# An LSTM with a residual on one core: weights loaded through several queues, scales per half of the state, a two-deep split and 512-wide input products

## The chip, the cores and the metric

The kernel runs on one core of a Trainium2 chip. The core has five engines that run side by side, each on its own stream of instructions and in order: PE (TensorE, matrix products), DVE (VectorE), ACT (ScalarE), POOL (GpSimd) and SP (SyncE). PE, DVE and ACT do nearly all of the work here; SP, ACT and POOL can start DMA transfers between device memory (HBM) and on-chip memory (SBUF). Products are summed in PSUM banks. The metric is the time of one execution on the device in microseconds (us); lower is better.

## What is computed

The reference is an LSTM over 512 steps for 16 sequences with 512 features and 512 hidden units, whose outputs are added to its input:

```python
xW = jnp.einsum('ntd,dg->ntg', x, Wx) + b        # 16 x 512 x 2048

def step(carry, xw_t):
    prev_h, prev_c = carry
    a = xw_t + prev_h @ Wh                       # Wh: 512 x 2048
    i = jax.nn.sigmoid(a[:, :Hdim])
    f = jax.nn.sigmoid(a[:, Hdim:2 * Hdim])
    o = jax.nn.sigmoid(a[:, 2 * Hdim:3 * Hdim])
    g = jnp.tanh(a[:, 3 * Hdim:])
    next_c = f * prev_c + i * g
    next_h = o * jnp.tanh(next_c)
    return ((next_h, next_c), next_h)
...
x = x + hs
```

Everything is float32. `x` is (16, 512, 512), the first h is `cond_1024` (16, 512), the first c is zero. A step needs the h of the step before, so the 512 steps are a chain.

## The kernel before

**Precision.** Wh is split into three float16 parts `wq0`, `wq1`, `wq2` (`split`, L377 to L387): a part is rounded on ACT, the remainder is taken on DVE, and so on. A power-of-two scale S, with its reciprocal RS, keeps the parts in range. It is found per partition from the largest absolute value (`amax`, L360, then nine small operations up to L375). h is likewise written in float16 parts (`parts`), scaled by S (the `scale` operation, L258), and the history of h is scaled back by RSL on ACT (`unscale`, L299). The first step alone multiplies float32 h by float32 Wh (`first_products`, L193).

**Tiles.** A product has the 32 columns of a small stationary operand (h or x, transposed) and streams 256 columns of weights. Four such products, j = 0 to 3, run side by side in the four column groups of the array and write partitions 32j to 32j+31. The state is handled in two halves, a and b, and each half's gates have two PSUM banks, used in alternate steps. The input product x Wx of two steps at a time, q, goes to one of four `xb` banks, started with the bias (`put_bias`, L147, on ACT), added up by `project` (L157, on PE) in two halves e of 256 columns, and copied into the gates' banks by `seed` (L167, on ACT) two steps ahead.

**Order.** Nothing is scheduled automatically. Each engine runs what is issued to it in the order of the program text. `STEP_PE` gives PE's order in a step: eight products for each of twelve names such as `q3aa` (part 3 of Wh, half a of h, gates of half a), then `x0` to `x3`, four input products each, for the pair of steps that begins four steps later, or three. `STEP` gives the order of DVE and ACT: turn the gates (`turn`, a transpose on DVE, L216), fold the parts together (`fold`, L223), tanh and sigmoid (ACT), `mix`, `cell`, tanh of the cell, then the new h in parts (`p1`, `copy`, `p2`, `rem`, `p2r`, L276 to L290) and its history (`h`, L270). Of a step's twelve names, the eighth, `q2ba`, is the last that the gates of half a need; it needs `p2r_b` of the step before (L290), the last DVE operation of half b.

**Before the first step.** SP's queue loads Wh (16 transfers of 256 KB, L128: row block c, quarter j, into partitions 32j to 32j+31), the first h (`h_in`, 4), the first block of x (`xs`, 8, L138), Wx (16) and the next x. ACT's queue loads the bias (8, L334). DVE takes the maximum of each of Wh's four row blocks c, finds the scale, turns the first h and x, and then ACT and DVE split Wh in eight pieces (4 blocks c, 2 halves e), each piece's chain started after the last one's. PE clears its eight banks with float32 products (L356), projects q = 0 and 1 as Wx lands, waits for the `seed` copies, which stand behind the split on ACT's stream, and runs the first step's products.

**At the end.** Each pair of steps p has a residual: transpose on DVE (L308), add on POOL (L309). After every fourth pair, SP writes 8 transfers of 32 KB (L315).

Of the kernel before, what the change touches and what calls it, by code (L numbers as in the profile page):

```python
# [14 lines left out]
P = 128  # L15
Q = 32
# [6 lines left out]
STEP_PE = "q3aa q3ab q1ab q1aa q2aa q3ba q1ba q2ba q2bb q1bb q2ab q3bb x0 x1 x2 x3"  # L23
# [8 lines left out]
def lstm_residual(ctx: ExitStack, tc: tile.TileContext, x, h0, wx, wh, b, out):  # L32
# [67 lines left out]
    wx_j = wx_sb.rearrange("p c (e g j w) -> p c e j g w", e=2, g=2, j=NJ)  # L100
# [4 lines left out]
    zero = const.tile([1, G * P], FP, tag="zero", name="zero")  # L105
    amax = const.tile([P, NK], FP, tag="amax", name="amax")
    top = const.tile([P, 1], FP, tag="top", name="top")
    bits = const.tile([P, 2], FP, tag="bits", name="bits")
    sc = const.tile([P, 5], FP, tag="sc", name="sc")
    S, RS, RS2, RSL = (sc[:, i : i + 1] for i in range(4))  # L110
# [13 lines left out]
    def load_w(dst, w, c):  # L124

        for j in range(NJ):
            r0 = j * P + c * Q
            nc.sync.dma_start(out=dst[j * Q : (j + 1) * Q, c], in_=w[r0 : r0 + Q])  # L128
# [3 lines left out]
    def load_xs(s):  # L132

        xs[s] = xsp.tile([P, XP, P], FP, tag="xs", name=f"xs_{s}")
        for j in range(NJ):
            for r in range(S2):
                p0 = j * Q + r * N
                nc.sync.dma_start(  # L138
                    out=xs[s][p0 : p0 + N],
                    in_=x[:, s * XB + r : (s + 1) * XB : S2, j * P : (j + 1) * P],  # L140
                )
# [4 lines left out]
    def put_bias(q):  # L146
        nc.scalar.copy(xb[q % NXB], bias)  # L147
# [6 lines left out]
    def project(q, c, e):  # L154

        for j in range(NJ):
            nc.tensor.matmul(  # L157
                xb[q % NXB][j * Q : (j + 1) * Q, (1 - e) * GU : (2 - e) * GU],
                lhsT=xT[q][:, c],
                rhs=wx_j[:, c, e, j],  # L160
                start=False,
                stop=(c == NK - 1),
                skip_group_check=True,
            )
# [75 lines left out]
    def act(t, op, h):  # L240
# [16 lines left out]
        elif op == "scale":  # L257
            nc.scalar.mul(new("os", t, h, [P, 2 * N]), v["so", h], S)  # L258
# [38 lines left out]
    def unscale(p):  # L297
        hs[p] = work.tile([P, P], FP, tag="hs", name=f"hs_{p}")
        nc.scalar.mul(  # L299
            hs[p], hist[p // XP][:, p % XP].rearrange("p c m -> p (c m)"), RSL  # L300
        )

    def residual(p):
        s, i = divmod(p, XP)
        if i == 0:
            ob[s] = outp.tile([P, XP, P], FP, tag="ob", name=f"ob_{s}")
        hb = work.tile([P, P], FP, tag="hb", name=f"hb_{p}")
        nc.vector.transpose(hb, hs[p])  # L308
        nc.gpsimd.tensor_tensor(ob[s][:, i], hb, xs[s][:, i], ALU.add)  # L309
        if i < XP - 1:  # L310
            return
        for j in range(NJ):
            for r in range(S2):
                p0 = j * Q + r * N
                nc.sync.dma_start(  # L315
                    out=out[:, s * XB + r : (s + 1) * XB : S2, j * P : (j + 1) * P],
                    in_=ob[s][p0 : p0 + N],
                )
# [4 lines left out]
    warm = const.tile([1, 1], FP, tag="warm", name="warm")  # L323
    nc.vector.memset(zero, 0.0)
    nc.vector.memset(h_in, 0.0)
    for c in range(NK):
        load_w(wh_sb, wh, c)
    for j in range(NJ):
        nc.sync.dma_start(out=h_in[j * Q : j * Q + N], in_=h0[:, j * P : (j + 1) * P])
    load_xs(0)  # L330
    b_j = b.rearrange("(o e g j w) -> j e o g w", o=1, e=2, g=2, j=NJ)
    for j in range(NJ):
        for e in range(2):
            nc.scalar.dma_start(  # L334
                out=bias[j * Q : (j + 1) * Q, (1 - e) * GU : (2 - e) * GU].rearrange(
                    "p (g w) -> p g w", g=2
                ),
                in_=b_j[j, e].broadcast_to([Q, 2, P]),
            )
    for c in range(NK):  # L340
        load_w(wx_sb, wx, c)
# [11 lines left out]
    nc.scalar.activation(warm, zero[:, 0:1], AF.Sigmoid)  # L353

    for bank in xb + gates[0] + gates[1]:
        nc.tensor.matmul(bank, lhsT=zero[:, :P], rhs=zero, start=True, stop=True)  # L356


    for c in range(NK):
        nc.vector.tensor_reduce(  # L360
            amax[:, c : c + 1], wh_sb[:, c], mybir.AxisListType.X, ALU.max, apply_absolute_value=True
        )
    nc.vector.tensor_reduce(top, amax, mybir.AxisListType.X, ALU.max)
    nc.vector.tensor_scalar(
        bits[:, 0:1].bitcast(I32), top.bitcast(I32), EXP, None, ALU.bitwise_and
    )
    nc.vector.tensor_scalar(
        bits[:, 1:2].bitcast(I32), top.bitcast(I32), EXP, EXP, ALU.bitwise_and, ALU.bitwise_xor
    )
    nc.vector.tensor_scalar(sc[:, 4:5], bits[:, 1:2], 2.0**13, 1.0, ALU.mult, ALU.min)  # L370
    nc.vector.tensor_scalar(RS, sc[:, 4:5], 2.0**-15, None, ALU.max)
    nc.vector.tensor_scalar(RS2, RS, 0.5, None, ALU.mult)
    nc.vector.tensor_scalar(RSL, RS, 1.0 / LO, None, ALU.mult)
    nc.vector.tensor_scalar(sc[:, 4:5], bits[:, 0:1], 2.0**-14, 1.0, ALU.mult, ALU.max)
    nc.vector.tensor_scalar(S, sc[:, 4:5], 2.0**15, None, ALU.min)  # L375

    def split(c, e):  # L377

        w = wh_sb[:, c, e * GH : (e + 1) * GH]
        f = [q[:, c, (1 - e) * GH : (2 - e) * GH] for q in wq]  # L380
        nc.scalar.mul(f[0], w, RS2)  # L381
        r1 = tmp.tile([P, GH], FP, tag="r1", name=f"r1_{c}_{e}")
        nc.vector.scalar_tensor_tensor(r1, w, RS, f[0], ALU.mult, ALU.subtract)  # L383
        nc.scalar.copy(f[1], r1)  # L384
        r2 = tmp.tile([P, GH], FP, tag="r2", name=f"r2_{c}_{e}")
        nc.vector.tensor_tensor(r2, r1, f[1], ALU.subtract)  # L386
        return lambda: nc.scalar.mul(f[2], r2, LO)  # L387

    nc.vector.transpose(hT0.rearrange("p c m -> p (c m)"), h_in)
    for q in range(2):  # L390
        turn_x(q)
    last = None
    for c in range(NK):
        for e in range(2):
            todo = split(c, e)
            if last:
                last()
            last = todo
            if (c, e) == (0, 0):
                for q in range(2):  # L400
                    put_bias(q)
    last()
    for q in range(2):
        for c in range(NK):
            for e in range(2):
                project(q, c, e)
    for t in range(2):
        for h in range(2):
            seed(t, h)
# [3 lines left out]
    for t in range(T):  # L413
# [4 lines left out]

        for op in STEP_PE.split():
            if op[0] == "x":  # L420
                i = int(op[1:])
                if q < NP:
                    project(q, 2 * half + i // 2, i % 2)
            elif t:
                products(t, int(op[1]), "ab".index(op[2]), "ab".index(op[3]))
            elif op[1] == "3":
                first_products("ab".index(op[2]), "ab".index(op[3]), hT0)
# [7 lines left out]
        if t % 2:  # L435
            unscale(t // 2)
# [40 lines left out]
```

## Time and profile before

| | |
|---|---|
| median of 3 runs | 2319.54 us (2317.95 to 2319.73) |
| the profiled execution: its time | 2319.52 us |
| its span, first to last instruction | 2317.7 us |
| granted TensorE clock, mean | 0.997 |
| busy: PE, PEld, DVE, ACT, POOL | 98%, 80%, 85%, 77%, 5% |
| first `turn` of the first step, last `turn_a` | at 70.42 us, at 2307.26 us |

The span is 1.8 us shorter than the execution's time. A row of the profile's groups gives line, engine, operation, tiles and shapes, the count, the busy time and the mean duration of one in ns; behind the second bar stands the engine's idle time just before, and what ended it. A row of the timeline gives start and duration in us; an idle time and its releaser stand in brackets. "PE" rows are matrix products, "PEld" rows are loads of the stationary operand, and rows on "SPq" or "ACTq" are DMA transfers being issued. A float32 product shows as two records. Products run four abreast and are pipelined, so the duration of a record is not the spacing of records.

### The profile page before, as it was taken

How to read it: one execution, taken by the hardware profiler on the slowest of the kernel's cores; microseconds unless marked ns; L12 is line 12 of the kernel's file. 1: busy time of each engine (PE TensorE's matmuls, PEld its weight loads, DVE VectorE, ACT ScalarE, POOL GpSimd, SP SyncE). 2: the span in 40 equal slices, each digit the busy share in tenths (PEclk: the TensorE clock that was granted, in tenths of full speed). 3: DMA queues.
4: the chain of work that ended last, by engine and by line, in shares of the span. 5: the costliest groups of instructions: out<-in, count | busy, mean ns of one | idle time of the engine just before them, and what ended most of it. 6: DMA issues, size and time to landing. Idle time of an engine off the chain costs nothing.

```text
span 2317.7 us, 153753 instructions
## 1 busy us (share of the span) xinstructions
PE 2263.9 (98%) x65584; PEld 1862.2 (80%) x65584; DVE 1958.8 (85%) x11808; ACT 1791.7 (77%) x7704; POOL 117.6 (5%) x264
## 2 busy tenths in 40 slices
PE   4899999999999999999999999999999999999997
PEld 1788888888888888888888888888888888888886
DVE  4788888888888888888888888888888888888887
ACT  3777777777777777777777777777777777777776
POOL 0000000000000000000000000000000000000000
PEclk9999999999999999999999999999999999999999
DMA  7000000000000000000000000000000000000000
GB/s 164 8 18 23 16 20 23 16 20 22 14 22 23 13 23 22 13 23 22 13 22 21 15 23 18 17 23 18 18 22 18 18 23 15 21 23 15 21 18 13
DMA packets 84907, 52.13 MB, mean 22 GB/s; under 512 B 17088, under 2 KB 83200, under 8 KB 83200
## 3 DMA queue, kind: packets, MB, share of 16 engines
q1 hardware_dynamic: 83584, 42.04, 7.9%
q8 instruction: 516, 8.45, 1.6%
q14 instruction: 167, 1.37, 0.2%
q10 hardware_dynamic: 640, 0.26, 0.1%
HBM read 25.46 MB, written 16.78 MB: 18 GB/s over the span
## 4 chain that ended last, share of the span: by engine, by line
PE 96%; DVE 1%; DMA 1%; ACT 1%; issue 0%; ACTq 0%; SPq 0%; POOLq 0%; POOL 0%; DVEq 0%
PE gates L180 58%; PE xb L157 38%; DMA wh_sb<-in_L_cond_Wh_dram 1%; DVE r L383 0%; ACT wq L381 0%; ACT wq L387 0%; PE gates L193 0%; ACT wq L384 0%; DMA bias<-in_L_cond_b_dram 0%; ACTq L334 0%; DVE gt L216 0%; DMA xs<-in_x_dram 0%; SPq L138 0%; DVE r L386 0%; ACT xb L147 0%
## 5 line engine op out<-in xcount | busy, mean ns | idle before, releaser
L180 PE MATMUL gates<-wq,parts 128*32 128x256 f16 x49056 | 1452.1, 273 | 5.3 <-DVE parts L276 4.2
L180 PEld LDWEIGHTS <-parts 128*32 128x32 f16 x49056 | 1306.3, 96 | 155.3 <-DVE parts L276 5.8
L157 PE MATMUL xb<-wx_sb,xT 128*32 128x256 f32 x16384 | 987.0, 380 | 27.1 <-DMA wx_sb<-in_L_cond_Wx_dram 27.1
L157 PEld LDWEIGHTS xb<-wx_sb,xT 128*32 128x32 f32 x16384 | 554.0, 110 | 270.3 <-ACT wq L381 20.2
L216 DVE STREAM_TRANSPOSE gt<-gates 128x192 f32<-128x192 f32 x1024 | 392.1, 383 | 237.0 <-PE gates L180 176.2
L250 ACT ACTIVATE gc<-pre 128x32 f32<-128x32 f32 x1022 | 235.0, 230 | 327.8 <-DVE pre L223 314.8
L167 ACT ACTIVATE gates<-xb,mask 128x256 f32<-128x256 f32 x1024 | 451.5, 441 | 0.0
L258 ACT ACTIVATE os<-so,sc 128x32 f32<-128x32 f32 x1024 | 329.1, 321 | 16.7
L280 ACT COPY parts<-parts 128x32 f16<-128x32 f16 x1022 | 214.5, 210 | 132.1 <-DVE parts L276 132.1
L223 DVE SCALAR_TENSOR_TENSOR pre<-gt 128x96 f32<-128x96 f32 x1024 | 254.2, 248 | 0.0
L252 ACT ACTIVATE sif<-pre 128x64 f32<-128x64 f32 x1024 | 245.5, 240 | 0.0
L216 DVE STREAM_TRANSPOSE gto<-gates 128x64 f32<-128x64 f32 x1024 | 230.3, 225 | 0.0
L309 POOL TENSOR_TENSOR ob<-hb,xs 128x128 f32<-128x128 f32 x256 | 116.6, 456 | 2193.6 <-DVE hb L308 1927.7
L256 ACT ACTIVATE so<-preo 128x32 f32<-128x32 f32 x1024 | 226.7, 221 | 0.0
L290 DVE SCALAR_TENSOR_TENSOR parts<-rem,parts 128x32 f16<-128x32 f32 x1022 | 196.6, 192 | 35.5
L268 ACT ACTIVATE tch<-gc 128x32 f32<-128x32 f32 x1024 | 226.3, 221 | 0.1
L223 DVE SCALAR_TENSOR_TENSOR preo<-gto 128x32 f32<-128x32 f32 x1024 | 193.0, 188 | 17.5
L282 DVE SCALAR_TENSOR_TENSOR parts<-parts,hist 128x32 f16<-128x32 f16 x1022 | 192.8, 189 | 17.7
L260 DVE TENSOR_TENSOR pr<-sif,gc 128x64 f32<-128x64 f32 x1022 | 205.6, 201 | 0.0
L276 DVE TENSOR_TENSOR parts<-os,tch 128x32 f16<-128x32 f32 x1022 | 196.7, 192 | 0.0
L266 DVE TENSOR_TENSOR gc<-pr 128x32 f32<-128x32 f32 x1024 | 192.9, 188 | 0.0
L270 DVE SCALAR_TENSOR_TENSOR hist<-os,tch 128x32 f32<-128x32 f32 x1024 | 189.6, 185 | 0.3 <-ACT tch L268 0.3
(42 smaller groups left out, 685.4 us busy)
## 6 DMA issues: line engine op xcount, KB each, us to landing
xs<-in_x_dram SPq DMA_DIRECT2D x512, 32.0 KB, 2.6
out_dram<-ob SPq DMA_DIRECT2D x512, 32.0 KB, 2.5
wh_sb<-in_L_cond_Wh_dram SPq DMA_DIRECT2D x16, 256.0 KB, 7.6
wx_sb<-in_L_cond_Wx_dram SPq DMA_DIRECT2D x16, 256.0 KB, 8.7
bias<-in_L_cond_b_dram ACTq DMA_DIRECT2D x8, 32.0 KB, 3.3
h_in<-in_cond_dram SPq DMA_DIRECT2D x4, 8.0 KB, 6.9
```

Of the source, the lines that this page charges most:

```text
L157: nc.tensor.matmul(xb[q % NXB][j * Q : (j + 1) * Q, (1 - e) * GU : (2 - e) * GU], lhsT=xT[q][:, c], rhs=wx_j[:, c, e, j], start=False, sto ...
L167: nc.scalar.mul(gates[h][t % 2][:, :GU].rearrange("p (g u) -> p g u", g=G), xb[t // 2 % NXB].rearrange("p (g h u) -> p h g u", g=G, h=2)[: ...
L180: nc.tensor.matmul(g[j * Q : (j + 1) * Q, :GU], lhsT=a[:, cc, k * N : (k + 2) * N], rhs=wq_j[i - 1][:, 2 * kh + cc, h, j], start=False, st ...
L216: nc.vector.transpose(gt.rearrange("p b m -> p (b m)"), gates[h][t % 2][:, b0 * Q : b1 * Q])
L223: nc.vector.scalar_tensor_tensor(pre.rearrange("p g (c n) -> p (g c) n", c=2), gt[:, :, (1 - t % 2) * N : (2 - t % 2) * N], 1.0 / LO, gt[: ...
L250: nc.scalar.activation(gc[h][:, 0], v["pre", h][:, 0], AF.Tanh)
L252: nc.scalar.activation(new("sif", t, h, [P, 2, 2 * N]), v["pre", h][:, 1:3], AF.Sigmoid)
L256: nc.scalar.activation(new("so", t, h, [P, 2 * N]), v["preo", h][:, 0], AF.Sigmoid)
L258: nc.scalar.mul(new("os", t, h, [P, 2 * N]), v["so", h], S)
L260: nc.vector.tensor_tensor(new("pr", t, h, [P, 2, 2 * N]), v["sif", h], gc[h], ALU.mult)
L268: nc.scalar.activation(new("tch", t, h, [P, 2 * N]), gc[h][:, 1], AF.Tanh)
L280: nc.scalar.copy(slots(t, h, 2), slots(t, h, 0))
```

## The change

- **Loads.** Wh's quarters j = 0 and 2 are issued by SP, j = 1 and 3 by ACT. The first x, then the first h, then the bias are issued by POOL. Wx is cut in two column parts, 32 transfers of 128 KB, half on SP and half on POOL, and lands with its column halves swapped; `project` takes a quarter's four runs of 128 columns in one access pattern.
- **Scale.** Instead of one scale per partition there are two, one for each half of h (row blocks 0 and 1, row blocks 2 and 3). The last block's bound is a sum of absolute values on ACT instead of a maximum on DVE.
- **Split.** A piece is in five steps (0, 2, 4 on ACT, 1, 3 on DVE), written out so that piece n+1's remainder and piece n+2's first part are issued inside piece n. Block 2's maximum is inside piece 1, block 3's bound and the second scale inside piece 2; the bias goes into `xb` inside pieces 3 and 4.
- **First step.** The input products of q = 0 and 1 are issued inside piece 4, 16 products with zeros follow them on PE, and the first step's seeds are issued inside piece 6.
- **x products.** `project` streams 512 columns instead of 256: two names per step instead of four.
- **Banks** are cleared with float16 zeros. DVE's first transposes come ahead of its first maximum.
- **End.** `unscale` has one instruction per half of h. The last pair's residual is written by itself, on SP and ACT; the three pairs before it are written when the third is done.

```diff
-STEP_PE = "q3aa q3ab q1ab q1aa q2aa q3ba q1ba q2ba q2bb q1bb q2ab q3bb x0 x1 x2 x3"
+STEP_PE = "q3aa q3ab q1ab q1aa q2aa q3ba q1ba q2ba q2bb q1bb q2ab q3bb x0 x1"
...
-    def load_w(dst, w, c):
+    def load_w(dst, w, c, dmas, parts=1):
+        n = G * H // parts
         for j in range(NJ):
             r0 = j * P + c * Q
-            nc.sync.dma_start(out=dst[j * Q : (j + 1) * Q, c], in_=w[r0 : r0 + Q])
+            for e in range(parts):
+                a = parts - 1 - e
+                dmas[j % 2].dma_start(
+                    out=dst[j * Q : (j + 1) * Q, c, a * n : (a + 1) * n],
+                    in_=w[r0 : r0 + Q, e * n : (e + 1) * n],
+                )
...
-    def project(q, c, e):
+    def project(q, c):
         for j in range(NJ):
             nc.tensor.matmul(
-                xb[q % NXB][j * Q : (j + 1) * Q, (1 - e) * GU : (2 - e) * GU],
+                xb[q % NXB][j * Q : (j + 1) * Q],
                 lhsT=xT[q][:, c],
-                rhs=wx_j[:, c, e, j],
+                rhs=wx_j[:, c, j],
...
-    def unscale(p):
...
+    def unscale(p, h):
+        if h == 0:
+            hs[p] = work.tile([P, NK, Q], FP, tag="hs", name=f"hs_{p}")
+        a = slice(2 * h, 2 * h + 2)
+        nc.scalar.mul(hs[p][:, a], hist[p // XP][:, p % XP, a], RSL[h])
...
+        if p == NP - 1:
+            put(s, i, i + 1, [nc.sync, nc.scalar])
+        elif p == NP - 2:
+            put(s, 0, i + 1, [nc.sync])
+        elif i == XP - 1:
+            put(s, 0, XP, [nc.sync])
...
+    for c in range(NK):
+        load_w(wh_sb, wh, c, (nc.sync, nc.scalar))
+    load_xs(0, nc.gpsimd)
...
-        nc.sync.dma_start(out=h_in[j * Q : j * Q + N], in_=h0[:, j * P : (j + 1) * P])
-    load_xs(0)
+        nc.gpsimd.dma_start(out=h_in[j * Q : j * Q + N], in_=h0[:, j * P : (j + 1) * P])
...
-            nc.scalar.dma_start(
+            nc.gpsimd.dma_start(
                 out=bias[j * Q : (j + 1) * Q, (1 - e) * GU : (2 - e) * GU].rearrange(
...
-        load_w(wx_sb, wx, c)
+        load_w(wx_sb, wx, c, (nc.sync, nc.gpsimd), 2)
...
+    def bound(c):
+        if c == NK - 1:
+            junk = tmp.tile([P, G * H], HP, tag="junk", name="junk", bufs=1)
+            nc.scalar.activation(junk, wh_sb[:, c], AF.Abs, accum_out=amax[:, c : c + 1])
+        else:
+            nc.vector.tensor_reduce(
...
+    def scales(h):
+        nc.vector.tensor_tensor(
+            top[:, h : h + 1], amax[:, 2 * h : 2 * h + 1], amax[:, 2 * h + 1 : 2 * h + 2], ALU.max
+        )
...
+    NH = 2 * NK
     for q in range(2):
         turn_x(q)
...
+    nc.vector.transpose(hT0.rearrange("p c m -> p (c m)"), h_in)
+    bound(0)
+    bound(1)
+    scales(0)
+    split(0, 0)
+    split(1, 0)
+    split(0, 1)
+    for n in range(NH):
+        if n == 1:
+            bound(2)
+        if n == 2:
+            bound(3)
+            scales(1)
+        if n + 1 < NH:
+            split(n + 1, 1)
+        split(n, 2)
+        split(n, 3)
+        if n + 2 < NH:
+            split(n + 2, 0)
+        split(n, 4)
+        if n in (3, 4):
+            put_bias(n - 3)
+        if n == 4:
+            for c in range(NK):
                 for q in range(2):
-                    put_bias(q)
...
+                    project(q, c)
+            for _ in range(16):
+                zeros(xb[3], False)
+        if n == 6:
+            for h in range(2):
+                seed(0, h)
+    for h in range(2):
+        seed(1, h)
     put_bias(2)
     turn_x(2)
```

`scales` has six small DVE operations behind the maximum, where the code before had eight behind its reduction; `split(n, k)` issues the same operation as before for each k.

## Prediction

> **What bounds the kernel now.** I read the page's chain first, then the groups, then timelines of three places: the loop, its last steps, the start.
>
> ```profile
> PE 96%; DVE 1%; DMA 1%; ACT 1%; issue 0%; ACTq 0%; SPq 0%; POOLq 0%; POOL 0%; DVEq 0%
> ```
>
> The chain says that the loop is PE's. It is a tie, which the last steps show, because they have no input products:
>
> ```profile
> 2290.45 1.91 PE L157 MATMUL xb<-wx_sb,xT 128*32 128x256 f32 x32
> 2292.18 2.82 PE L180 MATMUL gates<-wq,parts 128*32 128x256 f16 x96
> 2296.38 2.98 PE L180 MATMUL gates<-wq,parts 128*32 128x256 f16 x96 [1.38 <-DVE parts L276]
> 2300.75 2.98 PE L180 MATMUL gates<-wq,parts 128*32 128x256 f16 x96 [1.39 <-DVE parts L276]
> ```
>
> Without x, PE idles 1.38 us per step, yet 2296.38 to 2300.75 is 4.37. Now DVE's `turn_a`, in the middle of the run and at its end:
>
> ```profile
> 901.97 0.38 DVE L216 STREAM_TRANSPOSE gt<-gates 128x192 f32<-128x192 f32 x1 [0.38 <-PE gates L180]
> 906.33 0.38 DVE L216 STREAM_TRANSPOSE gt<-gates 128x192 f32<-128x192 f32 x1 [0.37 <-PE gates L180]
> ```
> ```profile
> 2302.90 0.38 DVE L216 STREAM_TRANSPOSE gt<-gates 128x192 f32<-128x192 f32 x1 [0.59 <-PE gates L180]
> 2307.26 0.38 DVE L216 STREAM_TRANSPOSE gt<-gates 128x192 f32<-128x192 f32 x1 [0.38 <-PE gates L180]
> ```
>
> 4.36 us with x, 4.36 without. The recurrence sets it: `turn_a`, then DVE and ACT up to `p2r_b` (3.76), then `q2ba` on PE and back (0.6). PE's own sum is next: fours of L180 records start every 0.1092 us, fours of L157 every 0.2158; 24 x 0.1092 + 8 x 0.2158 = 4.347, 15 ns under the median period of 4.362. The 511 periods from 70.42 to 2307.26 sum to 2236.84, 7.9 more than 511 x 4.362: 59 steps that run late.
>
> So what is left is 70.4 us ahead of the first `turn_a`, and 8.4 behind the last. The start's timeline:
>
> ```profile
> 0.73 4.74 ACTq L334 DMA_DIRECT2D bias<-in_L_cond_b_dram  x8
> 0.74 15.07 SPq L128 DMA_DIRECT2D wh_sb<-in_L_cond_Wh_dram  x16
> ...
> 11.02 2.29 DVE L360 TENSOR_REDUCE amax<-wh_sb 128x1 f32<-128x2048 f32 x1 [8.75 <-DMA wh_sb<-in_L_cond_Wh_dram]
> ...
> 24.92 2.29 DVE L360 TENSOR_REDUCE amax<-wh_sb 128x1 f32<-128x2048 f32 x1 [2.38 <-DMA xs<-in_x_dram]
> ...
> 28.24 1.15 ACT L381 ACTIVATE wq<-wh_sb,sc 128x1024 f16<-128x1024 f32 x1 [21.24 <-DMA xs<-in_x_dram]
> ...
> 48.36 6.58 PE L157 MATMUL xb<-wx_sb,xT 128*32 128x256 f32 x80 [2.85 <-DMA wx_sb<-in_L_cond_Wx_dram]
> ...
> 64.90 1.52 ACT L167 ACTIVATE gates<-xb,mask 128x256 f32<-128x256 f32 x4
> 65.38 5.49 PEld L193 LDWEIGHTS gates<-wh_sb,hT 128*32 128x32 f32 x128 [10.91 <-ACT gates L167]
> ```
>
> Wh is in by 24.9, the split runs from 28.2 to 65.0 (eight pieces every 4.39), the seeds wait behind it, and PE, done with x at 54.9, waits 10 us for them. The split is the path.
>
> **The change, part by part.**
>
> **Wider x.** 1024 cycles pass at once instead of twice 512. A spacing of 0.2158 is 512/2.4 GHz plus 2.5 ns, so a step's x costs 4 x 0.4292 = 1.717 instead of 1.727: 10 ns on PE. The recurrence covers all of it: 0. If PE set the period it would be 508 x 10 ns = 5.1 us gained. It can't lose while PE stays under 4.362 (4.337 now).
>
> **`unscale` in halves.** 128x128 takes 390 ns, `scale` on 128x32 321; so 128x64 about 345, twice 690: 0.3 us more on ACT in every second step. ACT idles 0.7 before its `tanh_a`, seed b behind it feeds PE a step later: 0. Exposed, it would be 256 x 0.3 = 77 us.
>
> **Wh over SP and ACT.** SP's second issue stood from 1.1 to 4.5 while ACT issued the bias; that goes, some 3.4 us. The rate is in doubt. Both ways matter: in the packets, the typical 8 KB of Wh takes 540 to 620 ns, the quickest 309, and the stream moves 1 MB per 4.66 us (225 GB/s). The Trainium skill, "SBUF — State Buffer", section "Can I just issue two DMAs to hit both halves?", speaks against the change: two transfers to different halves measured 6% more than one. By the rule Wh's first half is in at 1.8 + 2.1 MB / 239 GB/s = 10.6; by the quickest packet at about 6.5. Neither decides, as follows; I take the rule.
>
> **POOL's queue.** 8 transfers of x, 4 of h, 8 of bias, then 16 of Wx stand on it, one behind another. The trace has no DMA issued by POOL. Nearest is ACT's queue, 0.59 each (8 in 4.74). The skill's "DMA: Bandwidth & Descriptors", section "Latency and other measured facts", gives such a transfer about 1 us to its first byte, for descriptors that POOL's cores write in software. I take p = 1.0 us each, as POOL differs in kind from ACT's queue; ends 0.55 and 1.5 (the upper is my assumption). DVE's transposes of x and h now stand ahead of its maxima, so the maxima and all of the split wait for the twelfth: 0.7 + 11 x 1.0 + 3.5 to land (xs took 2.6, beside Wh more) = 15.2; at p = 0.55 it is 10.3, still behind Wh's first block. Behind the 36 issues stand only POOL's four clears of `parts` (0.7), wanted by the first step's `p1_a` at some 61: covered, unless p passes 1.6.
>
> **Start of the split.** 15.2 + 0.35 (turn h) + 2 x 2.29 (maxima) + four small operations of 0.19 = 20.9, against 28.24. Call it T.
>
> **The split two deep.** A piece has 3.0 of ACT (spacings 1.04, 0.95, 0.96) and 2.5 of DVE. Its period is copy 0.95, remainder on DVE 1.30 with hand-over (the next multiply lies beside it), last part 0.96: 3.25 instead of 4.39. To the second `put_bias`: first two steps 2.5, five pieces 16.2, block 3's bound on ACT 1.95 (2048 elements, from 1.05 for 1024), block 2's maximum 2.29 and the scale 0.9 on DVE, biases 1.1: T + 25 = 45.9. Wx does not hold this up: Wh and Wx are 8.4 MB, at 225 GB/s in by 41, the last POOL issue at 0.7 + 36 = 37, landed 40.
>
> **First products under the split.** PE projects when the bias is in. Its rows at 48.36 show four groups per 1.72 at first and twice that after 4.2 us, so 14 groups of 1024 cycles cost 5 x 0.855 + 9 x 0.43 = 8.2, the zeros 16 x 0.215 = 3.4, three quarters of the first products 24 x 0.109 + 0.35 = 3.0: T + 39.6 = 60.5. ACT is nearly as late: its two seeds wait for the projections (T + 33.5), and behind them stand piece 7, two seeds and a bias, to T + 39; `tanh_a` wants it at T + 40.3. Without PE's 4.2 slow us it ends 2 us sooner. First `turn_a`: 60.5 instead of 70.4, **-9.9 us**. Eight bank clears in f16 lie in PE's idle time: 0.
>
> **The end.** SP issues eight at 0.46, the last at 2314.89, of which the span's end follows 2.8 later. Four on SP beside four on ACT end 1.8 sooner: **-1.8**; if they took turns, 0.
>
> **The late steps.** PE reads 224 instructions a step instead of 256. If the 7.9 us come from that, an eighth goes, 1.0; the other 10 ns of slack in 59 steps are 0.6. I take 0.
>
> Sum: -9.9 - 1.8 = -11.7. The profiled time is 2319.52 (span 2317.7 + 1.8), the median 2319.54, so **2308**.
>
> **Rivals.**
>
> (a) *POOL is cheap* (p up to 0.7). At 0.55 T = 10.3 + 5.7 = 16, first `turn_a` 55.6: -14.8 - 1.8: about 2303; under 0.4 Wh's second block (11 + 2.29 + 0.75 = 14) takes over: 2301. For it: nothing else is on POOL, ACT manages 0.59. Against it: software. 0.24.
>
> (b) *PE sets the step.* The chain's 96%, and `q3aa` starts without a gap. Then 5 us more: 2303. Against it the steps without x. 0.08.
>
> (c) *POOL is the new bound, the time is longer.* Wx's last transfer lands at 0.7 + 36 p + 2.5; behind it 2.0 of x, 3.4 of zeros, 3.0: 11.6 + 36 p. From p = 1.52 this passes the split's path (9.9 + 11 p + 39.6), at 1.68 the gain is gone, at 1.81 the time is 4.6 us over. With p = 2: 83.6, +13.2 - 1.8 = 2331. For it: 36 transfers on a queue that has none now. 0.07.
>
> (d) *It does not do what it says*: the queues move nothing sooner, p is 1.5 to 1.8, and the pipelined split is spent on waiting for POOL: 2315 to 2323. 0.08.
>
> The forecast (p 0.7 to 1.5): 0.53.
>
> **How the numbers follow.** 0.2% is 4.6 us, about the least that a measurement of this kernel can tell from no change. The forecast's own range is p = 1.4 (T = 25.3, -5.5 - 1.8: 2312) to 0.7 (T = 17.6, 2304). The range takes in (a) and (b), with PE's 2 us, down to 2299, and up to 2315. Faster: (a), (b) and the forecast, 0.85. Same: (d), 0.08. Slower: (c), 0.07.
>
> **What would show it.** Right: POOL's issues about 1 us apart, DVE's first maximum held by `h_in`, ACT's first L381-like multiply near 21, pieces 3.25 apart, first `turn_a` near 60, and a median period still at 4.36. Wrong: a first maximum that waits for Wh; a projection that waits for Wx; a period under 4.35 (then b) or over 4.37 (ACT or PE's new form has become late, a case without a share in my chances).

## The result and the profile after

| | before | after |
|---|---|---|
| median (runs) | 2319.72 us (2317.95 to 2320.66, 7) | 2312.22 us (2311.23 to 2313.33, 7) |
| first multiply of the split, on ACT | 28.24 | 31.44 |
| first `turn_a` | 70.42 | 73.45 |
| from there to the last `turn_a`, 511 periods | 2236.84 | 2229.43 |
| median period; periods over it by more than 0.02 us (the "late" steps) | 4.362; 58 | 4.358; 20 |
| from the last `turn_a` to the span's end | 10.4 | 8.5 |
| span | 2317.7 | 2311.4 |

The ratio is 0.9969, with an interval of 0.9958 to 0.9981. The forecast was 2308 us in a range of 2299 to 2315, so the time lies inside it. The way to it was not the one forecast: the start, which should have become 9.9 us shorter, became 3.0 longer, and the loop, which should not have changed, became 7.4 shorter. Only the end did as forecast (1.9 shorter). (The prediction counts 59 late steps before; by the threshold of the table they are 58.)

The start first. This is the timeline of the kernel changed: start and duration in us, then engine, line, operation; in brackets the idle time before it and what ended that.

```profile
0.74 13.96 ACTq L132 DMA_DIRECT2D wh_sb<-in_L_cond_Wh_dram  x8
0.74 13.65 SPq L132 DMA_DIRECT2D wh_sb<-in_L_cond_Wh_dram  x8
...
1.31 4.21 POOL L145 DMA_DIRECT2D xs<-in_x_dram  x8 [0.86 <-POOLq L518]
...
10.47 0.51 POOL L342 DMA_DIRECT2D h_in<-in_cond_dram  x1 [4.96 <-DMA xs<-in_x_dram]
...
22.68 0.50 DVE L159 STREAM_TRANSPOSE xT<-xs 128x128 f32<-128x128 f32 x2 [20.65 <-DMA xs<-in_x_dram]
...
26.15 0.31 DVE L431 STREAM_TRANSPOSE hT<-h_in 128x128 f32<-128x128 f32 x1 [2.97 <-DMA h_in<-in_cond_dram]
26.39 4.45 DVE L381 TENSOR_REDUCE amax<-wh_sb 128x1 f32<-128x2048 f32 x2
...
31.44 2.19 ACT L414 ACTIVATE wq<-wh_sb,sc 128x1024 f16<-128x1024 f32 x2 [15.21 <-DVE sc L401]
...
55.60 8.32 PE L163 MATMUL xb<-wx_sb,xT 128*32 128x512 f32 x56 [1.87 <-ACT xb L154]
...
63.85 4.25 PE L368 MATMUL xb<-zero 1*128 1x512 f16 x16
...
68.03 6.36 PE L199 MATMUL gates<-wh_sb,hT 128*32 128x128 f32 x128
73.45 0.38 DVE L222 STREAM_TRANSPOSE gt<-gates 128x192 f32<-128x192 f32 x1 [7.00 <-PE gates L199]
```

POOL issues a transfer in 0.5 us, half of what the forecast took. But the x transfers issued from 1.31 on are all in only by 22.68, and the ninth of POOL's transfers, the first of h, stands until 10.47 because it waits for one of the first eight to land. The last of h is in just before its transpose starts at 26.15, and DVE's maxima stand behind that transpose. The page's list of issues has the same in its last column, the median us from issue to landing (count and KB each before it):

```profile
xs<-in_x_dram SPq DMA_DIRECT2D x504, 32.0 KB, 2.2
...
wx_sb<-in_L_cond_Wx_dram POOLq DMA_DIRECT2D x16, 128.0 KB, 6.8
xs<-in_x_dram POOLq DMA_DIRECT2D x8, 32.0 KB, 13.2
```

The same 32 KB take 2.2 us on SP's queue in the loop and 13.2 on POOL's beside Wh. At the other end of the start, the windows (us, length, busy us and count of PE, PEld, DVE, ACT and POOL, then the granted clock) say why the first products took 6.36 us:

```profile
64.00:66.00 2.00, 2.00 (x10) 0.84 (x9) 0.99 (x1) 0.97 (x2) 0.00 (x0) 1.00 0.01 4
66.00:68.00 2.00, 2.00 (x7) 0.52 (x5) 0.45 (x2) 1.74 (x4) 0.00 (x0) 0.68 0.00 0
68.00:70.00 2.00, 2.00 (x41) 1.82 (x44) 0.00 (x0) 0.53 (x2) 0.00 (x0) 0.50 0.00 0
70.00:72.00 2.00, 2.00 (x44) 1.85 (x40) 0.00 (x0) 0.00 (x0) 0.00 (x0) 0.50 0.00 0
```

PE was busy throughout, with the 16 products of zeros, and the clock still fell to a half just ahead of the products that needed it.

The chain of the kernel changed is PE's as before, and the period in its middle too is 4.36 (the two rows of `turn_a`):

```profile
PE 97%; DMA 2%; DVE 0%; ACT 0%; issue 0%; ACTq 0%; POOLq 0%; POOL 0%; SPq 0%
```
```profile
902.20 0.38 DVE L222 STREAM_TRANSPOSE gt<-gates 128x192 f32<-128x192 f32 x1 [0.37 <-PE gates L186]
...
906.55 0.38 DVE L222 STREAM_TRANSPOSE gt<-gates 128x192 f32<-128x192 f32 x1 [0.37 <-PE gates L186]
```

So the 7.4 us lie elsewhere: 5.4 in the late steps (the excess over the median period was 7.9 and is 2.5), 2.0 in a median that is 4 ns lower. What makes a step late, the trace of before shows in step 277, which took 4.80:

```profile
1285.41 0.82 PE L180 MATMUL gates<-wq,parts 128*32 128x256 f16 x21
1286.41 2.25 PE L180 MATMUL gates<-wq,parts 128*32 128x256 f16 x75 [0.19 <-issue]
```

PE stops inside the gates' products, after the 21st record of 96, and no semaphore holds it ("issue"). In steps 260 to 281 these pauses come at number 37, 36, 35, 34, 33, 32, then 28, 27, 24, 23, 21, 18, 17 of the 96: one place earlier in each step of 128 products, so every 127 products. One queue in the page's list has a count that fits (packets, MB, share); before, then after:

```profile
q8 instruction: 516, 8.45, 1.6%
```
```profile
q8 instruction: 452, 7.41, 1.4%
```

Its packets are 16 KB each, in the loop of the kernel before one per 4.3 us. PE's records of products, 65,584 before and 57,400 after, come to 127 per packet both times. I read this queue as PE's own program, fetched in blocks of some 127 products with their 127 loads. (Products are counted in records here and below: a float32 product counts twice.) The Trainium skill, "Runtime: NRT & Kernel Launch", section "Instruction fetch mechanics", describes such blocks of 16 KB, 256 instructions, and calls the cost of crossing into the next one mostly hidden. Here it is hidden in most steps only. In the kernel before, with 128 products a step, a block's end creeps through the step by one product, so that for 10 to 20 steps on end it lies in the stretch where a pause makes a step late (rows of late steps at 134 to 148, 262 to 281, 390 to 410: 128 apart). In the kernel changed a step has 112 products; the end jumps 15 places per step and comes back after 17 steps (15 blocks of 127 are 1905 products, 17 steps are 1904). Nine of its 20 late steps are 304, 321, 338, 355, 372; 449, 466, 483, 500. Not every late step is of this kind: 211 and 467 are late, by 0.17 to 0.20, in every profile of the kernel changed and of its variants below, whether a step has 112, 120 or 128 products; what delays those two was not looked for.

### The profile page after: what moved, and what is told of

It is laid out like the page before. It is cut to its first block, busy times and chain, and to the rows that moved or that the text cites. A ratio compares the mean times of both kernels' runs of the same rounds, so it can differ in the third digit from the quotient of the medians.

```text
span 2311.4 us, 137693 instructions
## 1 busy us (share of the span) xinstructions
PE 2249.4 (97%) x57400; PEld 1572.5 (68%) x57400; DVE 1952.7 (84%) x11812; ACT 1840.0 (80%) x7962; POOL 136.1 (6%) x300
## 4 chain that ended last, share of the span: by engine, by line
PE 97%; DMA 2%; DVE 0%; ACT 0%; issue 0%; ACTq 0%; POOLq 0%; POOL 0%; SPq 0%
PE gates L186 58%; PE xb L163 38%; DMA wh_sb<-in_L_cond_Wh_dram 1%; DMA wx_sb<-in_L_cond_Wx_dram 1%; DMA xs<-in_x_dram 0%; PE gates L199 0%; PE xb L368 0%; DVE r L424 0%; ACT wq L426 0%; ACT junk L379 0%; ACT wq L421 0%; DVE r L417 0%; DVE gt L222 0%; ACT xb L154 0%; ACTq L132 0%
## 5 line engine op out<-in xcount | busy, mean ns | idle before, releaser
L163 PE MATMUL xb<-wx_sb,xT 128*32 128x512 f32 x8192 | 978.0, 594 | 48.9 <-ACT xb L154 48.9
L163 PEld LDWEIGHTS xb<-wx_sb,xT 128*32 128x32 f32 x8192 | 264.1, 110 | 355.4 <-issue 303.8
## 6 DMA issues: line engine op xcount, KB each, us to landing
xs<-in_x_dram POOLq DMA_DIRECT2D x8, 32.0 KB, 13.2
```

The costliest lines, as they stand in the source:

```text
L163: nc.tensor.matmul(xb[q % NXB][j * Q : (j + 1) * Q], lhsT=xT[q][:, c], rhs=wx_j[:, c, j], start=False, stop=(c == NK - 1), skip_group_chec ...
```

## The experiments

Runs 1 to 4, 5 to 8 and 9 to 12 shared a chip each, with runs of the kernel before beside them (medians 2319.57, 2319.87, 2319.33). A run's time is compared with those on its own chip; starts are compared across chips, as they agree within 0.5 (run 5). All times below are in us; Wh "in" is the end of its last packet; "first", "loop" and "late" are the first `turn_a`, the 511 periods and the steps over the median by 0.02, from the profiled execution.

| run | median | ratio, interval | first | loop | median period; late |
|---|---|---|---|---|---|
| 1 turns late | 2302.78 | 0.9929, 0.9917 to 0.9941 | 59.48 | 2233.67 | 4.367; 24 |
| 2 no zeros | 2311.90 | 0.9968, 0.9956 to 0.9980 | 66.83 | 2235.00 | 4.367; 26 |
| 3 wide alone | 2315.88 | 0.9984, 0.9978 to 0.9991 | 70.14 | 2233.22 | 4.367; 22 |
| 4 before, pad | 2433.46 | 1.0493, 1.0479 to 1.0507 | 71.02 | 2351.20 | 4.602; 1 |
| 5 after again | 2315.34 | 0.9980, 0.9972 to 0.9987 | 73.92 | 2232.38 | 4.365; 22 |
| 6 both | 2296.11 | 0.9898, 0.9884 to 0.9911 | 53.16 | 2232.90 | 4.364; 23 |
| 7 half wide | 2319.99 | 1.0002, 0.9994 to 1.0010 | 73.54 | 2237.17 | 4.362; 60 |
| 8 three quarters | 2317.06 | 0.9987, 0.9980 to 0.9993 | 72.60 | 2232.86 | 4.362; 48 |
| 9 halves | 2293.82 | 0.9890, 0.9875 to 0.9904 | 51.31 | 2230.71 | 4.361; 11 |
| 10 two queues alone | 2319.83 | one run | 69.56 | 2238.08 | 4.362; 59 |
| 11 warm | 2293.04 | 0.9888, 0.9872 to 0.9905 | 51.24 | 2231.65 | 4.361; 19 |
| 12 real for zeros | 2310.47 | one run | 70.41 | 2229.64 | 4.361; 12 |

My theory of the start: what holds it is h on POOL's queue, as DVE does nothing before h has landed; and the zeros do not keep PE's clock up. Of the loop: theory F, the late steps come from the ends of instruction blocks, and the wider x changes how these run through the steps. Its rival S: the 10 ns of slack that the wider x gives PE in each step.

**1. The transposes of x and h moved behind the maxima**, where their wait holds nothing else up.

```diff
-    for q in range(2):
-        turn_x(q)
-    nc.vector.transpose(hT0.rearrange("p c m -> p (c m)"), h_in)
     bound(0)
...
+        if n == 3:
+            for q in range(2):
+                turn_x(q)
+            nc.vector.transpose(hT0.rearrange("p c m -> p (c m)"), h_in)
```

> The changed kernel, with one edit: DVE's transposes of the first x and the first h stand inside piece 3 of the split, no longer ahead of the first maximum. Theory A (the start was lost because all of DVE waits there for h, whose transfer on POOL's queue lands at 26 us): the first maximum starts when Wh's first block is in, near 8; ACT's first multiply moves from 31.4 to about 17, the first turn_a from 73.4 to 59 to 61, the time is 12 to 14 us under the changed kernel's, near 2299. Rival B (POOL's queue is the bound by its share of Wx, which lands at 45 us): the split starts early, but PE then waits for Wx, and the first turn_a moves by less than 5 us.

The first `turn_a` came at 59.48, 14.0 sooner than in the kernel changed. Its timeline has the maxima waiting for Wh, not for h:

```profile
8.65 2.29 DVE L381 TENSOR_REDUCE amax<-wh_sb 128x1 f32<-128x2048 f32 x1 [6.62 <-DMA wh_sb<-in_L_cond_Wh_dram]
...
14.57 2.29 DVE L381 TENSOR_REDUCE amax<-wh_sb 128x1 f32<-128x2048 f32 x1 [3.64 <-DMA wh_sb<-in_L_cond_Wh_dram]
...
17.46 2.19 ACT L414 ACTIVATE wq<-wh_sb,sc 128x1024 f16<-128x1024 f32 x2 [1.22 <-DVE sc L401]
```

The 14.0 us are those of the first multiply (31.44 to 17.46). The time was 4 us over what was expected of it, since this chip's loop is 4.2 longer than that of the chip on which the kernel changed was first run.

**2. The kernel changed without the 16 zero products** (they add zeros to a bank that `put_bias` overwrites later, so nothing reads them).

```diff
-            for _ in range(16):
-                zeros(xb[3], False)
```

> The changed kernel without the 16 products of zeros between the first input products and the first step's products. Theory A (products of one row of zeros don't count as activity; the clock falls at 66.7 while they run, and the first step's products pay for it): those products start near 64 at full clock, take 3.6 us instead of 6.4, first turn_a near 67.5, then ACT's stream is nearly the bound; 5 to 6 us faster. Rival (the zeros hold the clock up as far as it goes, and it falls without them sooner): the products start 4 us earlier but take 6.4 us all the same, or more, first turn_a near 69.5, 4 us faster or less.

The first products took 3.67 instead of 6.36 and the first `turn_a` came 6.6 sooner: 4.1 of zeros (the first products begin at 63.96, not 68.03) and 2.5 of half clock. ACT takes 1.1 of this back: the first tanh, which waited for DVE in the kernel changed (at 74.16), now starts right behind ACT's own stream, at 68.66, 5.5 sooner. The time against the first runs of the kernel changed shows little of the gain, since the loop on this chip is 5.6 longer, that 1.1 included. Run 6 shows it on one chip (below).

**3. The kernel before with the 512-wide products of x alone** (Wx in two parts for it, still on SP).

```diff
...
-                rhs=wx_j[:, c, e, j],
+                rhs=wx_j[:, c, j],
...
```

> The kernel before with the 512-wide x products alone (Wx is loaded by SP in two column parts, so that its halves land swapped). If the changed kernel's loop gained by these: the median period stays at 4.36, the late steps fall from 59 to about 20 and from 7.9 us to 2.5, the time is 5 us under the kernel before, near 2314.5. Rival (the loop's 7 us came from another part of the change, or from the chip that the profile was taken on): no more than 1 us.

It gained 3.7 at an unchanged start (70.14). Late steps fell from 58 to 22 and stand 17 apart (201, 218, 235, 252, 269; 329, 346, 363, 380, 397). The excess is 6.2 less than before's; a median period 5 ns longer took 2.5 of that back.

**4. The kernel before with four products of one row and 16 columns added per step**, to have 132 products a step at hardly any time.

```diff
+                    if i == 0:
+                        for j in range(NJ):
+                            nc.tensor.matmul(xb[q % NXB][j * Q : (j + 1) * Q, :16],
+                                lhsT=z16, rhs=z16[:, :16], start=False, stop=False, ...)
```

> The kernel before with four more products per step ahead of the x products: one row of zeros, 16 columns wide, side by side, added to the same bank. PE has 264 instructions per step instead of 256 and some 9 ns less slack (15 to 6). Theory F (a late step is one where PE's stream is held at the end of a block of instructions that it fetches; with 256 per step this end creeps by one product per step and stays for tens of steps where it hurts): the creep is ten times as quick, late steps fall to under half, 2 to 4 us faster than the kernel before. Theory S (late steps are pauses that PE's slack of 15 ns doesn't cover, and the wider x products gave it 10 ns more): slower, late steps as many or more, 0 to 5 us.

It decided nothing: the period rose to 4.602, so four such products cost 0.24 us, not some 9 ns. DVE's wait for the gates rose from 0.38 to 0.61 us per step, so I read that PE then sets the step, and no late step can show. Theory F is neither for nor against by this run.

**5. The kernel changed again**, as the reference on the chip of runs 6 to 8.

> The changed kernel again, on the chip of the next three, for its late steps and its median period there (4.358 in the first profile; 4.367 in three kernels of another chip). Expected: first turn_a near 73.4, a late step every 17 steps, 2311 to 2313 us. If the late steps are chance, their number and their spacing differ from the first profile's.

The change is worth 4.5 on this chip (2319.87 to 2315.34) where it was worth 7.5 on the first, so the time expected was missed, and the forecast's range too, by 0.3. Of the 20 late steps of the first profile 16 are late here as well (304, 321, 338, 355 and 372 among them), so they are not chance. The start is the same within 0.5; the loop is 2.95 longer, the median period 7 ns up. The kernel before did not move by more than 0.6 between chips.

**6. Runs 1 and 2 together.**

> The changed kernel with both edits: DVE's first transposes inside piece 3 of the split, and no zeros ahead of the first step's products. If both causes are as found: projections end near 50, held by Wx, the first step's products run at full clock, first turn_a 53 to 54, 19 us before the changed kernel's and 17 before the original's; 2296 to 2299 us. Rival (one is hidden behind the other: ACT's stream, whose last seeds wait for the projections, is then the bound): first turn_a at 57 or later, 2300 or more.

First `turn_a` at 53.16, 20.8 sooner than in run 5 on the same chip: the 14.0 of run 1 and the 6.6 of run 2 add up. The time, 2296.11, beats both kernels: 19.2 less than the kernel changed on the same chip.

**7. The kernel changed with x's products 256 wide again**, all else kept: 128 products a step.

```diff
...
-                rhs=wx_j[:, c, j],
+                rhs=wx_j[:, c, a, j],
...
```

> The changed kernel with the x products 256 columns wide again, as before (32 records instead of 16; PE has 256 instructions per step). Theory F (blocks of instructions end every 126.9 products, measured in both traces): late steps come in rows again, these rows 110 to 130 steps apart, 40 or more late steps, 3 to 6 us slower than the changed kernel on the same chip. Rival (the wide x has no part in the loop's gain): within 1 us.

The whole gain was gone: 2319.99, ratio 1.0002. Late steps were back at 60, with the rows of theory F: 93 to 141, 211 to 228, 246 to 266, 346 to 392, 467 to 506. Its page, beside the 452 of the kernel changed:

```profile
q8 instruction: 516, 8.45, 1.6%
```

**8. One name of x 512 wide, the other two 256**: 120 products a step, half of the slack.

```diff
-STEP_PE = "... q3bb x0 x1"
+STEP_PE = "... q3bb x0 x1 x2"
...
-                    project(q, 2 * half + int(op[1:]))
+                    i = int(op[1:])
+                    project(q, 2 * half + (i + 1) // 2, i - 1 if i else None)
```

> The changed kernel with one of a step's two x names 512 columns wide and the other as two of 256: 120 products per step instead of 112 or 128, PE's sum 4.342 instead of 4.337 or 4.347. Theory F: a block's end comes back to the same place of the step after 18 steps (18 x 120 = 2160 = 17.02 x 126.9), so late steps are 18 or a multiple of it apart, about 20 of them, time as the changed kernel's. Theory S (slack alone decides: 20 ns between 25 and 15): late steps in number between the two, no spacing of 18, 1 to 3 us slower than the changed kernel.

The late steps stand 18 apart (287, 305, 323; 342, 360, 378; 397, 415, 433, 451; 470, 488, 506). The spacing is that of the blocks: 18 steps are 2160 products, 17 blocks of 127 are 2159. That is F's forecast. But there are 48, between the 22 and the 60, and time and excess (3.9) lie between as well, which is what S forecast. So F gives the places, and S, or something else that goes with the width, has a part in how many of them turn into a late step.

**9. Run 6 with Wh's quarters dealt in halves**: SP's into partitions 0 to 63, ACT's into 64 to 127, instead of by turns. (The edit deals Wx in the same way.)

```diff
-                dmas[j % 2].dma_start(
+                dmas[j // 2].dma_start(
```

> The kernel of e6_both (no zero products, x's and h's transposes later) with Wh's quarters dealt out otherwise: SP loads the partitions 0 to 63 and ACT the partitions 64 to 127, where before SP had quarters 0 and 2 and ACT 1 and 3; Wx between SP and POOL alike. Theory A (the DMA engines carry 210 to 225 GB/s of 8 KB packets however the two queues share the partitions): Wh in by 23.6 us, packets of 8 KB still near 600 ns, the split's first multiply still at 17.5, the first turn_a at 53.2, the time within 2 us of 2296 (of that chip's own period). Theory B (two queues on different halves at once carry more, as was meant; the trace's quickest packet of 309 ns shows what one could do alone): by the 6% that the Trainium skill names, Wh in by 22.3 and the first multiply some 0.5 us sooner; by the quickest packet, Wh in by 13 to 14, the first multiply near 13, the first turn_a at 49 to 50.

Wh was in by 21.2 instead of 23.8, the first multiply at 16.12 instead of 17.49, the first `turn_a` 1.85 sooner. Windows of run 6, then of run 9, whose last column is GB/s:

```profile
8.00:10.00 2.00, 0.00 (x0) 0.00 (x0) 1.27 (x1) 0.00 (x0) 0.00 (x0) 1.00 1.03 205
10.00:12.00 2.00, 0.00 (x0) 0.00 (x0) 1.01 (x1) 0.00 (x0) 0.51 (x1) 1.00 1.09 233
```
```profile
8.00:10.00 2.00, 0.00 (x0) 0.00 (x0) 1.77 (x1) 0.00 (x0) 0.24 (x1) 1.00 1.09 272
10.00:12.00 2.00, 0.00 (x0) 0.00 (x0) 0.52 (x1) 0.00 (x0) 0.77 (x2) 1.00 0.95 225
```

Over the nine windows from 4 to 22 us the mean is 211 in run 6 and 238 in run 9. It is not the chip: run 11, on run 9's chip and dealt by turns, had 212 over the same stretch and Wh in by 23.6. Theory A, that the dealing does not matter, is wrong by 13%; theory B's larger figure, from a lone packet's 309 ns, is far off (8 KB packets took 0.54 in the median, in run 6 0.615).

**10. The kernel before with Wh alone over SP and ACT.**

```diff
-        load_w(wh_sb, wh, c)
+        load_w(wh_sb, wh, c, (nc.sync, nc.scalar))
```

> The kernel before with Wh alone moved to SP and ACT by turns (ACT's eight small issues of the bias stand behind it); x, h and Wx stay on SP behind Wh. Theory A (one queue already carries what the engines can): Wh in between 20 and 23.7 us (SP's pause of 3.4 us from 1.1 to 4.5 goes, as nothing else issues beside it), the rate still 210 to 225 GB/s, packets still 540 to 620 ns. Since SP has half of Wh's issues, x's first block and Wx move up with it: first multiply 2 to 4 us sooner than 28.24, first turn_a 67 to 70. Theory B (the second queue starved POOL's: it is what held h at 26.15 in the kernel changed): x and h land here within 4 us of Wh's end, as they share SP's queue. Theory C (two queues do carry more): Wh in by 13 to 16, first multiply near 20.

Wh was in by 21.4 (before 23.7), at some 220 GB/s against 229 (windows from 6 us on): no more per us, only SP's pause of the first 4.5 us gone. The first multiply came 2.3 sooner but the first `turn_a` only 0.9: x, which follows on SP, landed at 28.55 and held the first remainder. Here, on SP, h was in 2.2 us and x 7 us after Wh. In the ten profiles with h on POOL's queue it was in 2.3 to 2.7 us after Wh, in the kernel changed at 26.0, though issued there from 10.47 on. So theory B is not borne out as it stands: POOL's queue brought h hardly later after Wh than SP's did, but its earlier issue won nothing.

**11. Run 6 with 16 products of 128 rows set ahead of the projections**, while PE has nothing else to do. (The expectation says that they change the result; that is mistaken, `put_bias` overwrites their bank before it is used.)

```diff
+            for _ in range(16):
+                nc.tensor.matmul(xb[3], lhsT=wq[2][:, 1, GH : GH + P],
+                    rhs=wq[2][:, 1, GH : GH + G * P], start=False, stop=False, ...)
             for c in range(NK):
                 for q in range(2):
                     project(q, c)
```

> The kernel of e6_both with 16 products of 128 rows by 512 columns in f16, of a block of Wh's third part, set ahead of the projections, in PE's idle time before the bias is in (they add something to the fourth x bank, so the values of steps 6 and 7 and what follows them aren't the reference's). Theory A[...]: in e6_both the projections began at half clock at 41.66 and took 8.65 us to 50.3; with the clock raised before, 14 groups of 1024 cycles take 14 x 0.43 = 6.0, so they end near 47.7, and the first products and turn_a follow 2 to 2.6 us sooner: first turn_a 50.6 to 51.2, the time 2294 less or more what the chip's period makes of it. Rival (ACT's seeds set the first step): the projections end 2.6 us sooner, but the first tanh_a waits for ACT, which was free at 55.0 only, so turn_a comes sooner but tanh_a does not move, and the time stays at 2296.

The projections took 6.3 instead of 8.8. Rows of run 6, then of run 11:

```profile
49.74 0.81 ACT L173 ACTIVATE gates<-xb,mask 128x256 f32<-128x256 f32 x2 [1.53 <-PE xb L163]
...
54.99 0.24 ACT L256 ACTIVATE gc_init<-pre 128x32 f32<-128x32 f32 x1
```
```profile
34.66 5.43 PE L456 MATMUL xb<-wq 128*128 128x512 f16 x14
...
41.41 6.32 PE L163 MATMUL xb<-wx_sb,xT 128*32 128x512 f32 x56 [0.32 <-ACT xb L154]
...
48.35 3.70 PE L199 MATMUL gates<-wh_sb,hT 128*32 128x128 f32 x128 [0.62 <-ACT gates L173]
...
53.10 0.24 ACT L256 ACTIVATE gc_init<-pre 128x32 f32<-128x32 f32 x1
```

Fours of projections start 0.85 apart in run 6 until 46.9, where the trace has its first record of the clock, and 0.43 apart from there on; in run 11 they are 0.43 apart throughout. (The windows' clock column reads 1.00 ahead of the first record, so there the spacing tells more.) The first `turn_a` came 1.9 sooner than in run 6, and the first tanh with it (53.10 against 54.99). The rival is half right. In both runs this tanh follows ACT's own stream without idle time, some 1.2 after DVE had its input ready, so ACT does set the first step. But ACT's first seeds had waited 1.53 for the projections in run 6, and so ACT's stream moved too; in run 11 PE waits for a seed instead. At 2293.04 it and run 9 are the quickest seen. Both edits in one kernel were not tried.

**12. The kernel changed with the 16 zero products replaced by such products of 128 rows** (the same mistake in the expectation).

> The kernel changed, with each of the 16 zero products of one row (f16, 512 columns) ahead of the first step replaced by one of 128 rows of a block of Wh's third part (they add something to the fourth x bank, so the values of steps 6 and 7 and what follows them aren't the reference's). Theory A (products of one row, of zeros, don't hold the clock up, so the first products ran at half clock in the kernel changed: 6.36 us): the clock stays at 1.0 from the projections on, the first products take 3.6 to 3.7, the first turn_a comes at 70.4 to 71.2 instead of 73.45. Rival (the clock falls because of something else in that stretch, the wait for the gates' data or the count of products): the clock falls near 66.7 again and the first turn_a stays at 73 to 74.

The clock stayed up, in the windows of 66 to 70 us:

```profile
66.00:68.00 2.00, 2.00 (x28) 0.99 (x30) 0.56 (x2) 1.63 (x3) 0.00 (x0) 1.00 0.00 0
68.00:70.00 2.00, 2.00 (x84) 2.00 (x76) 0.00 (x0) 0.63 (x2) 0.00 (x0) 1.00 0.00 0
```

The first products took 3.70, the first `turn_a` came at 70.41, 3.0 sooner than in the kernel changed. So it is the products of one row of zeros that let the clock fall, and not the wait or the number of products.

## Why the prediction was right and wrong

The sum was -11.7, and the span shrank by 6.3. Term by term:

- **"The maxima and all of the split wait for the twelfth: 0.7 + 11 x 1.0 + 3.5 to land = 15.2": failed**, and it is the largest miss. The sign was right (h held the first maximum), the term was not one of issuing: p took a time to the first byte for a spacing of issues. POOL issues in 0.5, so the issues alone would have ended at 1.3 + 12 x 0.5 = 7.3. But its transfers wait for each other eight at a time, and beside Wh they take 12 to 13 us to land in the median. h was in at 26.0, the split began at 31.44 instead of 20.9: +10.5. All of the cases over p, rival (a) among them, moved the wrong variable: p was at its lower end, and the start was still late. Run 1 shows that nothing but this wait was in the way: 17.46 without it.
- **The split two deep, T + 25: held.** From the first multiply to the end of the second `put_bias` it took 24.1; pieces without a `put_bias` are 3.28 apart in run 6 (3.25 forecast).
- **"Three quarters of the first products 24 x 0.109 + 0.35 = 3.0": failed**, by 2.4 (68.03 to 73.45 is 5.4). The projections took 8.3 (8.2 forecast) at the two spacings forecast, but the sum then took full clock for granted. The zeros took 4.25 (3.4) and let it fall. With 0.9 won back in the split, T + 42.0 instead of T + 39.6. Runs 2 and 12 show both parts of this. That ACT is nearly as late was right too: without the zeros it is the later of the two by some 1.2 (runs 2, 6, 11).
- **Wh over two queues, "the rule": its size held, but the change is not the case it speaks of.** The forecast took the Trainium skill's 6% ("SBUF — State Buffer", section "Can I just issue two DMAs to hit both halves?"), against twice the rate by the quickest packet. That figure is for two transfers to different halves of the partitions. The change deals the quarters by turns, into one half at a time, and gained nothing: Wh was in by 23.6, before by 23.7. Dealt to both halves at once (run 9) the queues moved 238 GB/s, 4% over the 229 of the one queue before and near the 6%; by turns it was 211 (run 6), both with POOL's stream beside them. Without POOL's stream, by turns reached 220 (run 10). Whether halves help there too wasn't run.
- **The loop is a tie that the recurrence sets; the wider x is worth 0 by its 10 ns: held as far as the period goes.** Median periods were 4.358 to 4.367 with the wide x and 4.362 with the narrow one, so rival (b), 5 us by PE's rate, is not what happened. The 10 ns are right: fours of 512-wide products start 0.429 apart in the start of the kernel changed. (The 2.4 GHz and 2.5 ns in that sum follow from the prediction's two spacings: 256 columns or cycles more take 215.8 - 109.2 = 106.6 ns, and 109.2 less this leaves 2.6.)
- **"The late steps ... I take 0": failed**, by 5.4; the other 2.0 of the loop's gain lie in the median. The text named the cause, PE's instructions, and sized it by their share, an eighth of 7.9, before it took 0. But an eighth fewer instructions took away two thirds of the late steps. Their places follow from how a block of 127 products falls on a step of 128 or of 112, which could have been read from the trace of before: its late steps come in rows 128 apart, and the pauses shift by one product a step. Runs 3 and 7 show that the wide x brings the loop's gain: alone it is worth 3.7, and without it the change is worth nothing (1.0002). By which of its effects, they do not show.
- **The end, -1.8: held** (-1.9). The output's last issues are SP's and ACT's side by side. `unscale` in halves costs what was said and holds no step.

Three terms that held (split, end, period) would not have brought the number near. It came near by luck: a start 12.9 worse than forecast met a loop 7.4 better. On the chip of run 5 the same kernel lay just outside the range.

**Open:** why the median period of the wide form differs by chip: 4.358 on the first, 4.361 in runs 9, 11 and 12, 4.364 and 4.365 in runs 6 and 5, 4.367 in runs 1 to 3, where the narrow form has 4.362 in three profiles. It is worth up to 4.6 us and decides whether the change gains 4.5 or 7.5. Also open is what sets the number of late steps. The wide form changes three things at once: where the blocks end in a step, PE's 10 ns, and the loads of the stationary operand, 16 fewer per step (PEld is busy for 80% before, 68% after); run 8 changes all three. Nor is the number fixed by them: nine profiles with the wide x have 11 to 26. For the start, h and x ahead of Wh on SP's queue were not tried.

## What to carry to other kernels

An early wait on an in-order engine belongs behind whatever does not need it: three transposes ahead of the maxima cost 14 us, and moving them won twice what the whole change had. What a queue costs is not its issue time but the time to landing beside whatever else streams (0.5 and 13 us here). In a loop whose engines are tied, list the late steps and look at their spacing before any of them is called noise: here a step of 128 products, nearly a fetched block of 127, made them come in long rows.

## What the hardware showed

- POOL's queue: 0.48 to 0.57 us per issue, the ninth transfer waits for one of the eight before it; 32 KB landed after 13.2 us in the median beside two streams of 8 KB packets, h's 8 KB after 12.3.
- Sixteen products of one row of zeros didn't keep PE's clock up: after some 3 us of them (63.85 to 66.7) it fell to a half, with PE never idle; with 128 rows of weights it stayed (run 12). Whether the rows or the zeros decide wasn't separated.
- Four products of one row and 16 columns among those of 128 rows cost 0.24 us per step.
- One queue brings 16 KB per some 127 of PE's products; in the kernel before PE's pauses lie 127 products apart, of 0.1 to 0.45 us, though no semaphore holds it.
- Two queues writing to different halves of the partitions moved 238 GB/s, to quarters of the same half 211, POOL's stream included; one queue alone 229.
